# A bias product of 128 columns in place of 256, added behind the two-matrix product of its bank

## The chip, the cores and the metric

The kernel runs on one core of a Trainium2 chip. The metric is the device time of one execution in microseconds (us). Before the change three runs gave 2354.51, 2358.6 and 2351.19 us, median 2354.51.

TensorE multiplies a stationary operand (loaded by a weight load) by a moving operand and writes the result to an accumulator bank in PSUM. VectorE, ScalarE and GpSimd work on elements, SyncE (SP) issues transfers. In the profile PE is TensorE's matmul, PEld its weight load, DVE is VectorE, ACT is ScalarE and POOL is GpSimd.

## The reference

Two graph layers run over 16 graphs of 1024 nodes with 128 channels. The first is a gated network of four steps over the adjacency. The second, which the change touches, takes out some edges and then applies three SAGE passes and a linear head:

```
def _sage(x, adj, Wr, Wx, b, mf):
    deg = clip(sum(adj, axis=-1, keepdims=True), 1.0, None)
    agg = einsum('bij,bjd->bid', adj, x) / deg
    out = agg @ Wr + x @ Wx + b
    nrm = maximum(norm(out, axis=-1, keepdims=True), NORM_EPS)
    return out / nrm * mf[..., None]

h1 = bn(relu(sage(x,  adj_d, Wr1, Wx1, b1, mf)))
h2 = bn(relu(sage(h1, adj_d, Wr2, Wx2, b2, mf)))
h3 = bn(relu(sage(h2, adj_d, Wr3, Wx3, b3, mf)))
xc = concatenate([h1, h2, h3], axis=-1) * mf[..., None]
return (xc @ Wl + bl) * mf[..., None]
```

`bn` normalizes each channel over all graphs and nodes, so no graph's second pass can begin before the last graph's first pass has ended, and likewise for the third.

## The kernel before

The kernel is one program in five stages: the gated network together with the search for the edges to take out (to about 1330 us), the first pass of SAGE (to about 1890 us), the second pass (to about 2143 us), the third pass (to about 2282 us) and the head (to the end). `Sage.run` calls `first`, `second`, `third` and `last` in this order. Inside each stage, the order of the instructions on every engine is the order of the Python code: no scheduler moves them.

The batch normalization isn't applied to the data. `weights(l)` folds its scale into the weights of the next pass: `wr2` for the aggregate, and `wxp`, which holds two matrices beside each other, `Wx` of this pass and the head's part for the previous pass's output. Its shift gives a bias row: `r6` holds six rows in bfloat16, the bias of the aggregated and the plain term, each split into three parts so that their sum is exact. The matching factors of each node are in `rho`, six rows by 1024 nodes, so that the bias is a product with six rows. In `r6` only the first 128 columns are filled; the other 128 columns are set to zero once (L1276).

The work unit of the second and third passes is half a graph, 512 nodes, as four blocks of 128 nodes. `out_next(b, f)` (L1753) issues its products on TensorE:

- L1759, four products of the aggregate with `wr2`, into the bank `q_oa`.
- L1762, four bias products, with the block of `rho` stationary (6 by 128) and `r6` moving (256 columns), into the tile `q_ob`. That tile has two banks; blocks 0 and 1 share one, blocks 2 and 3 the other. The product of an even block carries the start flag, which opens its bank.
- L1765, four products of the block of `xt` with `wxp`, 256 columns in float32, which are added in the same banks. A float32 product is two records in the profile, a bfloat16 product is one. Columns 0 to 127 of a block are the pass's own term, columns 128 to 255 the head's share of the previous pass.

`chain(b, f)` (L1768) then scales the aggregate by the inverse degree (VectorE L1376 in the second pass, four ScalarE activations L1374 in the third), adds the own term (VectorE L1377), and forms the squares and their root on ScalarE (L1384, L1385). The head's share is added to an accumulator by VectorE (L1809 in the second pass, L1873 in the third), and this is what frees `q_ob`. `rows` (L1390 to L1395, VectorE) divides by the norm and applies the rectifier.

In the second pass, `slot_second(b, t)` lays out a graph in eight slots. `out_next` is in slots 0 and 3. In between TensorE turns the previous results by transposes (L1406) and aggregates the previous graph over its adjacency (L1798, float32r). The adjacency comes as bytes, unpacked by GpSimd, ScalarE and VectorE (L1749, L1751). The step that follows a unit's `out_next` is L1406 or L1798.

In the third pass, each of the 32 units i does on TensorE: the transposes (L1406) of unit i-3, then `out_next` of unit i. ScalarE copies the transposes (L1858), then does L1374, L1384 and L1385 of unit i. VectorE does `rows` of unit i-2, the statistics of unit i-3 (L1869), then L1377 and L1873 of unit i. At unit 8 a flag is formed on VectorE and TensorE (L1971 to L1977), and at unit 16 all engines load it. `q_oa`, `q_ob` and `s_tr` have two buffers there.

`load_layer` (L1716) issues on SP the loads of `q_rho`, `q_agi` and `q_xt` of a graph, in this order; each waits until the last reader of its buffer is done (two buffers in the second pass, three in the third).

The first pass has a similar sequence in `out_first` (L1565): L1571 (aggregate), L1573 (bias, six rows, 128 columns), L1576 (own term, 128 columns). It uses the same `r6`, columns 0 to 127. The head has bias products of 48 rows (L1907), behind L1899 or behind the 512-column L1903.

Of the kernel before, what the change touches and what calls it, by code (L numbers as in the profile page):

```python
# [9 lines left out]
BF = mybir.dt.bfloat16  # L10
# [11 lines left out]
P = 128  # L22
B = 16
N = 1024
C = 128
# [26 lines left out]
class Dilate:  # L52
# [15 lines left out]
    def __init__(self, ctx, tc, cst, adj, not_r):  # L68
        self.tc, self.nc, self.cst, self.adj, self.not_r = tc, tc.nc, cst, adj, not_r
        nc = self.nc  # L70
        pool = lambda name, **k: ctx.enter_context(tc.tile_pool(name=name, **k))
        self.one = pool("d_one", bufs=1)
        self.two = pool("d_two", bufs=2)
        self.small = pool("d_small", bufs=3)
        self.dram = pool("d_dram", bufs=1, space=DRAM)
        self.ps = pool("d_ps", bufs=1, space=PSUM)

        self.removed = [self.dram.tile([N, N], BF, name=f"rt{b}") for b in range(B)]

        self.coef = self.one.tile([B, ROW], F32, name="coef")
        nc.vector.memset(self.coef, 1.0)
        nc.vector.memset(self.coef[:, TAIL + 1:TAIL + 2], -1.0)
        nc.vector.memset(self.coef[:, TAIL + 2:TAIL + 3], -0.5)
        nc.vector.memset(self.coef[:, TAIL + 5:TAIL + 6], 2.0)  # L90
        self.stage = self.one.tile([P, B, ROW], BF, name="stage")
        for i, v in ((1, -8.5), (2, 1.0), (3, MAGIC), (4, -MAGIC), (5, 0.0)):
            nc.vector.memset(self.stage[:, :, TAIL + i:TAIL + i + 1], v)
        self.counts = self.one.tile([P, B, NB], F32, name="counts")
        self.free = {}
# [1101 lines left out]
class Sage:  # L1197
# [14 lines left out]
    def __init__(self, ctx, tc, cst, adj, not_r, summed, nodemask, W, vec, Wl, bl, out, bad):  # L1212
        self.tc, self.nc, self.cst = tc, tc.nc, cst
        self.adj, self.not_r, self.summed, self.out, self.bad = adj, not_r, summed, out, bad
        self.given = nodemask, W, vec, Wl, bl
        self.ctx = ctx
        pool = lambda name, **k: ctx.enter_context(tc.tile_pool(name=name, **k))
        self.one = one = pool("s_one", bufs=1)
        self.small = pool("s_small", bufs=2)
        dram = pool("s_dram", bufs=1, space=DRAM)  # L1220
        self.x1 = dram.tile([B, P, NB, C], F32, name="s_x1")
        self.at8 = dram.tile([B, 2, P, NB, HF], U8, name="s_at8")
        self.rt = dram.tile([B, 2, C, HF], F32, name="s_rt")
        self.ag = dram.tile([B, 2, C, HF], F32, name="s_ag")
        self.rho = dram.tile([B, 6, N], BF, name="s_rho")
        self.wr = one.tile([C, 3, C], F32, name="s_wr")
        self.wx = one.tile([C, 3, C], F32, name="s_wx")
        self.wl = one.tile([C, 3, C], F32, name="s_wl")

        self.vr = one.tile([10, C], F32, name="s_vr")  # L1230
        self.vt = one.tile([C, 10], F32, name="s_vt")
        self.part6 = one.tile([6, 3], F32, name="s_part6")

        self.graph = one.tile([3 * B, B], F32, name="s_graph")
        self.mask48 = one.tile([3 * B, N], BF, name="s_mask48")
        self.rdeg = one.tile([P, B, NB], F32, name="s_rdeg")
        self.stats = [one.tile([C, 2 * B, 6], F32, name=f"s_st{l}") for l in range(3)]
        self.ab = [one.tile([C, 2], F32, name=f"s_ab{l}") for l in range(3)]
        self.wr2 = one.tile([C, C], F32, name="s_wr2")
        self.wxp = one.tile([C, 2, C], F32, name="s_wxp")  # L1240
        self.r6 = one.tile([6, 2 * C], BF, name="s_r6")

    def load_given(self):

# [14 lines left out]
    def constants(self):  # L1259

        nc, ident, K = self.nc, self.cst["ident"], 3 * B
        const = self.const
        self.one16 = const([1, 1], 1.0, "s_one16", F16)

        self.sel01 = const([10, 3, 6], 0.0, "s_sel01")
        for i in range(3):
            nc.vector.tensor_copy(self.sel01[:, i, 3:], ident[:10, 3 * i:3 * i + 1].to_broadcast([10, 3]))
        self.ones = const([6, P], 1.0, "s_ones", BF)
        nc.vector.tensor_add(self.part6, ident[:6, 0:3], ident[:6, 3:6])
        self.part48 = const([K, 3], 1.0, "s_part48")  # L1270
        for base, m in ((0, 1), (B - 1, -1)):
            nc.gpsimd.affine_select(self.part48, self.part48, pattern=[[-m * B, 3]], compare_op=ALU.is_ge,
                                    fill=0.0, base=base, channel_multiplier=m)
        nc.vector.tensor_add(self.graph, ident[:K, :B], ident[:K, B:2 * B])
        nc.vector.tensor_add(self.graph, self.graph, ident[:K, 2 * B:K])
        nc.vector.memset(self.r6[:, C:], 0.0)  # L1276

        mask, junk = self.cst["mask"], self.wxp[:, 0, :].rearrange("p (a b) -> p a b", a=NB)
        nc.vector.scalar_tensor_tensor(junk, mask, 0.0, mask, op0=ALU.is_gt, op1=ALU.not_equal,
                                       accum_out=self.bad[:, BAD - 1:BAD])  # L1280

        drop = self.wr2
        nc.vector.tensor_copy(drop, ident)
        nc.vector.memset(drop[:1, :], -1.0)
        nc.vector.memset(drop[:1, :1], 0.0)
        nc.vector.memset(self.mask48[:B, :], 1.0)
# [13 lines left out]
    def const(self, shape, v, name, dt=F32):  # L1300
        t = self.one.tile(shape, dt, name=name)
        self.nc.vector.memset(t.bitcast(F32) if dt is FR else t, v)
        return t
# [30 lines left out]
    def weights(self, l, v):  # L1334

        nc = self.nc
        if l:
            self.batch_norm(l - 1)
            self.scaled(self.wr2, self.wr[:, l, :], l - 1)
            self.scaled(self.wxp[:, 0, :], self.wx[:, l, :], l - 1)  # L1340
            self.scaled(self.wxp[:, 1, :], self.wl[:, l - 1, :], l - 1)
            beta = self.small.tile([C, 2, 6], F32, name="s_beta")
            nc.vector.memset(beta, 0.0)
            for i in range(2):
                nc.vector.tensor_copy(beta[:, i, 3 * i:3 * i + 3], self.ab[l - 1][:, 1:2].to_broadcast([C, 3]))
            nc.tensor.matmul(v, beta[:, 0, :], self.wr[:, l, :], start=True, stop=False)
            nc.tensor.matmul(v, beta[:, 1, :], self.wx[:, l, :], start=False, stop=False)
        nc.tensor.matmul(v, self.sel01[:, l, :], self.vr, start=(l == 0), stop=True)
        self.parts(v, self.part6, self.r6[:, :C])

    def head_weights(self, ps):
        nc, K = self.nc, 3 * B
# [212 lines left out]
    def out_first(self, b, f):  # L1565
        nc, g = self.nc, self.g[b]
        pa = self.ps1.tile([P, 4, C], F32, name="p_oa")
        pb = self.ps1.tile([P, 4, C], F32, name="p_ob")
        ag = g["ag", f]
        for i in range(4):  # L1570
            nc.tensor.matmul(pa[:, i, :], ag[:, i * P:(i + 1) * P], self.wr[:, 0, :], start=True, stop=True)  # L1571
        for i in range(4):
            nc.tensor.matmul(pb[:, i, :], self.ones, self.r6[:, :C],  # L1573
                             start=(i == 0), stop=False)
        for i in range(4):
            nc.tensor.matmul(pb[:, i, :], g["xt", f][:, i * P:(i + 1) * P], self.wx[:, 0, :],  # L1576
                             start=False, stop=(i == 3))
        g["oa", f], g["ob", f] = pa, pb
# [174 lines left out]
    def out_next(self, b, f, ps):  # L1753
        nc, g = self.nc, self.g[b]
        pa = ps.tile([P, 4, C], F32, name="q_oa")
        pb = self.ps2.tile([P, 4, 2, C], F32, name="q_ob")
        for i in range(4):
            blk = slice(i * P, (i + 1) * P)
            nc.tensor.matmul(pa[:, i, :], g["agi"][:, f, blk], self.wr2, start=True, stop=True)  # L1759
        for i in range(4):  # L1760
            blk = slice(f * HF + i * P, f * HF + (i + 1) * P)
            nc.tensor.matmul(pb[:, i], g["rho"][:, blk], self.r6, start=(i % 2 == 0), stop=False)  # L1762
        for i in range(4):
            blk = slice(i * P, (i + 1) * P)
            nc.tensor.matmul(pb[:, i], g["xt"][:, f, blk], self.wxp, start=False, stop=(i % 2 == 1))  # L1765
        g["oa", f], g["ob", f] = pa, pb

    def chain(self, b, f, scalar=False):  # L1768
# [282 lines left out]
```

## Time and profile before

| what | value |
|---|---|
| median of three runs | 2354.51 us (2351.19 to 2358.6) |
| profiled execution: span | 2361.0 us |
| instructions in it | 35725 |
| TensorE matmul, busy | 2271.3 us, 96% |
| TensorE weight load, busy | 1567.2 us, 66% |
| VectorE, busy | 1905.5 us, 81% |
| ScalarE, busy | 1371.4 us, 58% |
| GpSimd, busy | 1027.0 us, 44% |
| L1765, 512 records | 133.0 us, mean 405 ns |
| L1759, 512 records | 71.4 us, mean 285 ns |
| L1762, 256 records | 40.1 us, mean 277 ns |
| L1573 (first pass), 128 records | 12.6 us, mean 217 ns |

The profile is of one execution, apart from the three timed runs, and only its span from first to last instruction is known. A record's length includes the time in which a matmul drains, while the next one already runs; what a matmul takes from TensorE is the distance from its start to the start of the next. In rows of the timeline the columns are: start and length in us, engine, line, operation, output and inputs, shape, number of records, and in brackets the idle time before it with the instruction that ended it. Names in the profile leave out the buffers' numbers, so `s_r` in the rows of L1762 and L1573 is `r6`. In a table by stretch, each engine's busy time stands with its number of instructions, then the granted TensorE clock as a share of full speed, the mean share of the transfer engines and the rate.

### The profile page before, as it was taken

The numbers are of one execution on the slowest core, as the hardware profiler recorded it, in microseconds if no ns is written. First come the engines' busy times: TensorE is split into PE (matmuls) and PEld (weight loads), VectorE is DVE, ScalarE is ACT, GpSimd is POOL, SyncE is SP. The second block draws the span as 40 slices with busy tenths as digits, with TensorE's granted clock in tenths as the row PEclk, the third lists the DMA queues.
The fourth block names the chain that finished last, engine by engine and source line by source line (L and its number), as shares of the span: only waits on it lengthen the run. The fifth ranks groups of instructions, "written<-read, shape, count | busy, mean of one in ns | idle before, by whom it ended". The sixth has DMA issues, their size and how long they took to land. (4 is left out here: it accounts for less than half of the span.)

```text
span 2361.0 us, 35725 instructions
## 1 busy us (share of the span) xinstructions
PE 2271.3 (96%) x11945; PEld 1567.2 (66%) x11945; DVE 1905.5 (81%) x4132; ACT 1371.4 (58%) x3206; POOL 1027.0 (44%) x964
## 2 busy tenths in 40 slices
PE   6999999999999999999999899999999989999987
PEld 4665655656665666656566577777777778887865
DVE  4998998988989989989889877777777566666777
ACT  3556565656465655556664556666566545555756
POOL 3236254253362452533532556666666435551002
PEclk9999999999999999999999899999999999999989
DMA  7327254363353372533640787778777277765414
GB/s 264 113 97 264 72 173 168 115 225 129 111 207 104 123 243 67 204 137 115 235 134 26 263 297 279 272 271 301 277 267 278 105 259 245 240 233 167 127 37 145
DMA packets 214406, 436.18 MB, mean 185 GB/s; under 512 B 59586, under 2 KB 80740, under 8 KB 214212
## 3 DMA queue, kind: packets, MB, share of 16 engines
q1 hardware_dynamic: 186244, 345.70, 42.2%
q0 software_dynamic: 23040, 83.90, 10.2%
q10 hardware_dynamic: 4928, 4.21, 0.6%
q8 instruction: 96, 1.57, 0.3%
q14 instruction: 98, 0.80, 0.1%
HBM read 324.49 MB, written 109.25 MB: 184 GB/s over the span
## 5 line engine op out<-in xcount | busy, mean ns | idle before, releaser
L1092 PE MATMUL h_g<-h_h,h_wh 128*128 128x512 f32 x768 | 397.9, 600 | 3.1 <-DVE h_r L1105 3.0
L1092 PE MATMUL h_g<-h_ms,h_wi 128*128 128x512 f32 x768 | 392.2, 593 | 0.0
L1492 POOL CAST p_b<-p_at 128x512 uint8<-128x512 f32 x256 | 257.1, 1024 | 124.2 <-ACT p_at L1485 124.2
L735 DVE TENSOR_TENSOR_SCAN f_rank<-f_a,f_first,f_pd 128x1024 f16<-128x1024 f32 x128 | 299.2, 2344 | 3.3
L1080 PE MATMUL h_g<-h_a,h_hi 128*128 128x512 f32 x1024 | 284.5, 418 | 5.7 <-DMA h_a<-in_adj_dram 5.5
L1092 PEld LDWEIGHTS h_g<-h_ms,h_wi 128*128 128x128 f32 x768 | 145.9, 190 | 183.6 <-issue 161.1
L1121 POOL TENSOR_TENSOR h_h<-h_zh,h_r 128x512 f32<-128x512 f32 x126 | 181.9, 1444 | 195.0 <-DVE h_r L1120 172.8
L1080 PE MATMUL h_g<-h_a,h_lo 128*128 128x512 f32 x1024 | 264.3, 395 | 0.0
L1485 ACT ACTIVATE p_at<-p_u,s_less 128x512 fp32r<-128x512 f32 x256 | 175.7, 688 | 146.2 <-PE p_u L1484 141.3
L1080 PEld LDWEIGHTS h_g<-h_a,h_hi 128*128 128x128 f32 x1024 | 188.6, 189 | 69.5 <-issue 20.1
L863 DVE SCALAR_TENSOR_TENSOR f_nr<-f_u,f_q,f_a 128x1024 bf16<-128x1024 f16 x128 | 183.5, 1450 | 57.4 <-ACT f_u L912 50.8
L1115 POOL TENSOR_TENSOR h_zh<-h_z,h_h 128x512 f32<-128x512 f32 x63 | 80.3, 1275 | 324.1 <-ACT h_z L1111 324.1
L1080 PEld LDWEIGHTS h_g<-h_a,h_lo 128*128 128x128 f32 x1024 | 190.2, 188 | 39.3
L1501 DVE SCALAR_TENSOR_TENSOR p_a<-p_a 128x1024 bf16<-128x1024 f32 x128 | 211.7, 1694 | 0.0
L1384 ACT ACTIVATE s_junk<-s_o 128x128 bf16<-128x128 f32 x384 | 113.8, 298 | 137.3 <-DVE s_o L1377 137.3
L1092 PEld LDWEIGHTS h_g<-h_h,h_wh 128*128 128x128 f32 x768 | 129.4, 191 | 86.1 <-issue 66.5
L1083 ACT COPY h_ms<-h_g 128x512 f32<-128x512 f32 x128 | 73.7, 576 | 174.3 <-PE h_g L1080 130.3
L1108 ACT ACTIVATE h_r<-h_r,h_bi 128x512 f32<-128x512 f32 x128 | 92.4, 722 | 138.8 <-DVE h_r L1107 138.8
L909 ACT ACTIVATE f_u<-f_rank,f_q 128x128 f16<-128x128 f16 (+7 forms) x128 | 110.6, 867 | 75.5 <-DVE f_rank L849 75.5
L1483 PE MATMUL p_u<-ident_b,p_a 128*128 128x128 bf16 x1024 | 145.4, 222 | 2.2 <-DMA p_a<-in_adj_dram 2.2
L1484 PE MATMUL p_u<-ident_b,p_nr 128*128 128x128 bf16 x1024 | 145.3, 222 | 0.0
L1765 PE MATMUL q_ob<-s_wxp,q_xt 128*128 128x256 f32 x512 | 133.0, 405 | 0.0
(258 smaller groups left out, 4950.0 us busy)
## 6 DMA issues: line engine op xcount, KB each, us to landing
h_a<-in_adj_dram POOLq DMA_DIRECT2D x128, 512.0 KB, 7.5
p_a<-in_adj_dram SPq DMA_DIRECT2D x128, 512.0 KB
f_a<-in_adj_dram SPq DMA_DIRECT2D x124, 512.0 KB
e_nr<-f_nr SPq DMA_DIRECT2D x128, 256.0 KB
p_nr<-e_nr SPq DMA_DIRECT2D x32, 1024.0 KB
s_at<-p_b SPq DMA_DIRECT2D x32, 512.0 KB
s_ag<-s_ag SPq DMA_DIRECT2D x64, 256.0 KB
q_agi<-s_ag SPq DMA_DIRECT2D x32, 512.0 KB
```

Source lines behind the costliest of these rows:

```text
L735: nc.vector.tensor_tensor_scan(out, a, other[:, 0, 0:1].to_broadcast([P, N]), start, op0=ALU.add, op1=ALU.bypass)
L863: nc.vector.scalar_tensor_tensor(nr, self.us[g], self.q[:, 2, g:g + 1], self.a[g], op0=ALU.not_equal, op1=ALU.is_ge)
L1080: nc.tensor.matmul(pm[f], part[:, j, :], st.adj[j][:, half[f]], start=(j == 0 and n == 0), stop=(j == NB - 1 and n == 1))
L1092: nc.tensor.matmul(pg, lhs, rhs, start=(i == 0), stop=(i == len(mm) - 1))
L1121: aid.tensor_tensor(h, zh, r, ALU.subtract)
L1384: self.nc.scalar.activation(junk, o[:, i, :], AF.Square, accum_out=ss[:, i:i + 1])
L1483: nc.tensor.matmul(pu[:, i * P:(i + 1) * P], a[:, blk, 1], ib, start=False, stop=False)
L1484: nc.tensor.matmul(pu[:, i * P:(i + 1) * P], nr[:, k, blk], ib, start=False, stop=(i == 3))
L1485: nc.scalar.activation(g["at"][:, j, cols], pu, AF.Relu, bias=self.less2)
L1492: self.nc.gpsimd.tensor_copy(g["b", f][:, j, :], g["at"][:, j, f * HF:(f + 1) * HF].bitcast(F32))
L1501: self.nc.vector.scalar_tensor_tensor(low, a, 0.0, a, op0=ALU.is_gt, op1=ALU.not_equal, accum_out=self.bad[:, c:c + 1])
L1765: nc.tensor.matmul(pb[:, i], g["xt"][:, f, blk], self.wxp, start=False, stop=(i % 2 == 1))
```

## The change

`r6` becomes 128 columns wide, and the memset of its second half goes. In `out_next` the two-matrix product L1765 comes in front of the bias product and carries the start flags; the bias product is 128 columns wide, goes to columns 0 to 127 of its block, and stands last, with the stop flags. The number of products is the same. Lines behind L1276 move up by one: in the changed kernel the products of `out_next` are L1758 (aggregate), L1761 (two matrices) and L1764 (bias).

```diff
@@ __init__ @@
-        self.r6 = one.tile([6, 2 * C], BF, name="s_r6")
+        self.r6 = one.tile([6, C], BF, name="s_r6")
@@ constants @@
-        nc.vector.memset(self.r6[:, C:], 0.0)
@@ weights @@
-        self.parts(v, self.part6, self.r6[:, :C])
+        self.parts(v, self.part6, self.r6)
@@ out_first @@
-            nc.tensor.matmul(pb[:, i, :], self.ones, self.r6[:, :C],
+            nc.tensor.matmul(pb[:, i, :], self.ones, self.r6,
                              start=(i == 0), stop=False)
@@ out_next @@
         for i in range(4):
+            blk = slice(i * P, (i + 1) * P)
+            nc.tensor.matmul(pb[:, i], g["xt"][:, f, blk], self.wxp, start=(i % 2 == 0), stop=False)
+        for i in range(4):
             blk = slice(f * HF + i * P, f * HF + (i + 1) * P)
-            nc.tensor.matmul(pb[:, i], g["rho"][:, blk], self.r6, start=(i % 2 == 0), stop=False)
-        for i in range(4):
-            blk = slice(i * P, (i + 1) * P)
-            nc.tensor.matmul(pb[:, i], g["xt"][:, f, blk], self.wxp, start=False, stop=(i % 2 == 1))
+            nc.tensor.matmul(pb[:, i, 0, :], g["rho"][:, blk], self.r6, start=False, stop=(i % 2 == 1))
         g["oa", f], g["ob", f] = pa, pb
```

## The prediction

> **What bounds the kernel now.** I read the page's list of groups first, then busy time by stretch, then the timeline of one unit on each engine, because one sum over 2361 us mixes stages with different limits. The two passes that change run from about 1895 to 2143 us and from 2145 to 2282 us.
>
> Busy time by stretch: the middle of the second pass, then a late stretch of the third.
>
> ```profile
> core 0: us, PE busy (x) PEld busy (x) DVE busy (x) ACT busy (x) POOL busy (x), PEclk, DMA share, GB/s
> 1905.00:2130.00 225.00, 223.31 (x1195) 184.02 (x1194) 149.93 (x274) 120.31 (x393) 110.91 (x90) 1.00 0.69 236
> 2218.00:2275.00 57.00, 56.40 (x356) 46.89 (x354) 46.60 (x106) 44.99 (x210) 0.00 (x0) 1.00 0.32 94
> ```
>
> TensorE looks full in both. Busy time can't say whether it is the bound in both, so next the timeline: one unit of the third pass on TensorE (start, length).
>
> ```profile
> 2202.19 1.06 PE L1759 MATMUL q_oa<-s_wr,q_agi 128*128 128x128 f32 x8
> 2203.18 0.61 PE L1762 MATMUL q_ob<-s_r,q_rho 6*128 6x256 bf16 x4
> 2203.71 2.00 PE L1765 MATMUL q_ob<-s_wxp,q_xt 128*128 128x256 f32 x8
> 2205.54 0.60 PE L1406 MATMUL s_tr<-ident,s_r 128*128 128x128 f32 x4
> 2205.98 1.06 PE L1759 MATMUL q_oa<-s_wr,q_agi 128*128 128x128 f32 x8
> ```
>
> A unit is 2205.98 - 2202.19 = 3.79 us with no idle time. The four bias products hold 2203.71 - 2203.18 = 0.53 us of it. Now ScalarE and VectorE in the same unit:
>
> ```profile
> 2198.96 0.31 ACT L1384 ACTIVATE s_junk<-s_o 128x128 bf16<-128x128 f32 x1 [0.76 <-DVE s_o L1377]
> ...
> 2200.27 0.21 ACT L1385 ACTIVATE s_ss<-s_ss 128x4 f32<-128x4 f32 x1
> 2200.38 0.57 ACT L1858 COPY s_r<-s_tr 128x512 f32<-128x512 f32 x1
> 2200.84 1.15 ACT L1374 ACTIVATE s_o<-q_oa,s_rdeg 128x128 f32<-128x128 f32 x4
> 2202.75 0.31 ACT L1384 ACTIVATE s_junk<-s_o 128x128 bf16<-128x128 f32 x1 [0.76 <-DVE s_o L1377]
> ```
> ```profile
> 2202.02 0.69 DVE L1377 TENSOR_TENSOR s_o<-q_ob,s_o 128x512 f32<-128x512 f32 x1 [0.35 <-ACT s_o L1374]
> ```
>
> This is a closed loop: four squares 1.31 us, root 0.11, copy 0.46, four scalings until L1377 starts 1.18, L1377 until the next square 0.73. That is 3.79 too, and ScalarE's only idle time is the wait for L1377, which itself waited for ScalarE. In this unit both are nearly tied: the bias bank is complete at 2199.92 + 2.00 = 2201.92 (L1765 of this unit started at 2199.92), L1374 ends at 2201.99. After ScalarE loses 0.76 us at the flag's load (near 2217 us) TensorE is ahead, and ScalarE's loop runs on its own:
>
> ```profile
> 2217.95 0.69 DVE L1377 TENSOR_TENSOR s_o<-q_ob,s_o 128x512 f32<-128x512 f32 x1 [0.35 <-ACT s_o L1374]
> ...
> 2270.99 0.69 DVE L1377 TENSOR_TENSOR s_o<-q_ob,s_o 128x512 f32<-128x512 f32 x1 [0.35 <-ACT s_o L1374]
> ```
>
> These are 14 units apart: 53.04 / 14 = 3.789 us. TensorE's pitch, from L1765 at 2203.71 and 18 units later at 2271.97, is 3.792 us. So the third pass is held by two loops of equal length, and the ScalarE loop contains no bias product. In the second pass the unit is 7.47 us (L1762 at 2014.09, 2021.54, 2029.04), TensorE is without gaps, ScalarE idles 2.4 to 3.5 us a unit and VectorE waits 0.58 and 0.77 us for TensorE's L1765: there TensorE alone is the bound.
>
> **What the Trainium skill says.** *TensorE: Matmul & The Clock Gate*, section Back-to-back issue gap, gives N / 2.4 + 2.5 ns between full-speed matmuls, about 109 ns for 256 columns and 56 for 128. The trace agrees: L1762's starts are 109 to 110 ns apart, L1573's (128 wide, also 6 rows) 55 to 56. The same page, step 1 of Step-by-step, says that a weight load is pulled ahead where row groups don't conflict. The trace fits: a 6-row load behind 128-row work starts only 202 ns after the last such matmul (pitch 112), while loads of equal height overlap. *PSUM — Partial Sum Buffer*, The four PSUM rules: a group's first matmul clears the has-written bits of its whole 2 KiB bank, so whichever product comes first must carry the start flag; the change moves it, two per tile as before. No trace shows these bits. The TensorE page's Part 1 has the clock halved after an idle window of some 3.4 us, free-running; here the granted clock was 0.50 from 2179.8 to 2186.6 us, after TensorE stood idle for 2.0 us.
>
> **The change part by part.** *Width.* There are 64 groups of four bias products, 32 in each pass. The first pass already has this shape:
>
> ```profile
> 1536.94 1.11 PE L1571 MATMUL p_oa<-s_wr,s_ag 128*128 128x128 f32 x8
> 1537.99 0.39 PE L1573 MATMUL p_ob<-s_r,s_ones 6*128 6x128 bf16 x4
> 1538.31 1.16 PE L1576 MATMUL p_ob<-s_wx,p_xt 128*128 128x128 f32 x8
> ```
>
> L1573 holds 1538.31 - 1537.99 = 0.32 us, L1762 holds 0.53: the difference is 4 x (109.5 - 56) = 0.214 us a group.
>
> *Place.* Entering the 6-row products costs 95 ns (207 instead of 112 after L1759; before L1907, behind a 512-wide product, 524 instead of 431: 93). Leaving costs 88 ns until the next load starts and 104 until it is done (L1765's first step is 320 instead of 216). Now L1765 follows L1759, equal rows, no switch; the switch in comes behind L1765, the switch out falls on L1406 or L1798. Two switches remain, about 0.29 us, as before. The switch out onto L1798 (fp32r) is shown nowhere: between 0 (hidden) and twice the 0.19; I take 0.19, as its load is as long. The ends are +-0.19 x 15 groups = +-2.9 us. But the bank completes sooner than TensorE moves on. From L1759's last start to completion it takes 2.74 us now (2.36 to the last L1765's start, and 0.38); then 0.11 + 7 x 0.216 + 0.31 + 0.18 + 0.22 = 2.33: 0.41 us earlier, of which 0.19 is the switch that now falls behind it.
>
> *Waits.* What waits for a free bank is now L1765, half a microsecond earlier in the unit; the bank was released 3.7 us before (L1873 of two units back), so nothing. The loads: L1762 no longer frees q_rho's buffer before L1765 frees q_xt's, so on SP's queue the load of q_rho, and q_agi behind it, issue 1.5 us later in the third pass (2203.81 and 2204.18 now, with q_xt at 2205.74). They are used four units, 15 us, later, and a load took 3.7 to 6.1 us from issue to landing in the busier second pass: nothing. Without that cover it would cost up to 1.5 us a graph. The removed memset (L1276, once, 112 ns on VectorE at 1323.9 us) is worth between 0 and 0.1 us, and I count 0; so is the smaller tile.
>
> *Second pass.* VectorE and ScalarE in turn need 14.94 - 0.77 - 0.58 = 13.59 us a graph, TensorE afterwards 14.94 - 0.43 = 14.51: still TensorE's. GpSimd's unpacked bytes are ready some 1.5 us before use. 32 x 0.214 = 6.8 us, and 0.2 because the tail hangs on the bank's completion: 7.0 us.
>
> *Third pass.* In steady state the next late thing is ScalarE's loop, which is already there: 0.004 us a unit for 14 units, 0.05 us, and TensorE idles 0.2 us a unit. It gains only where VectorE really waits for L1765 at half clock: at the start (L1377 at 2151.15) and behind the flag, where the wait of L1975 for VectorE has stopped TensorE.
>
> ```profile
> 2186.85 0.69 DVE L1377 TENSOR_TENSOR s_o<-q_ob,s_o 128x512 f32<-128x512 f32 x1 [5.12 <-PE q_ob L1765]
> ```
>
> At half clock 4 x (214 - 107) = 0.43, and 0.23 for the earlier completion: 0.66 at each, with the next unit's share some 0.7. Twice 0.7 = 1.4 us.
>
> Sum 7.0 + 1.4 = 8.4 us. The profiled execution's span, 2361.0, becomes 2352.6; it stands 6.5 us over the median of the runs, 2354.51, and I take the same 8.4 us from that: **2346.1 us**.
>
> **Rivals.** *Full gain.* The ScalarE loop is not rigid and the third pass gives its 6.8 us as well: 7.0 + 6.8 + 0.7 = 14.5, 2340.0 us. For it: TensorE's 56.40 of 57 us. Against: the fourteen units at 3.789. *Half eaten.* One or two more half-clock pieces, since TensorE now has idle time in the third pass and waits longer at the flag. A unit at half clock was 7.07 us (L1406 at 2179.49 and 2186.56) instead of 3.79, 3.3 more; one piece of 6.8 us costs 3.4: gain 5.0, 2349.5 us. The same end is reached if leaving onto L1798 costs double (gain 5.5). *Slower.* The clock stays halved in the third pass, because TensorE waits in each unit: 3.3 us a unit. Break-even is 8.4 / 3.3 = 2.5 units; with 5 units 2354.5 + 8.1 = 2362.6 us. Against: from 2293 to 2350 us TensorE has 1.5 us idle in 57 and the clock is 1.00. *No effect of the width*, if the 93 ns weight load set the pitch: 2353, spoken against by L1573's 56 ns.
>
> **How the numbers follow.** My case 0.62, own range 2343 to 2349 (three runs of the kernel before span 7.4 us); full gain 0.12; half eaten or no width effect 0.22; slower 0.04. About 0.3%, 7 us, is what a measurement here can tell. My case lies just beyond it and reaches beyond it three times in four: 0.47, with 0.12 and 0.01 makes faster 0.60; same 0.36; slower 0.04. Range 2340 to 2351 takes in the full gain and most of the half eaten.
>
> **What would show it.** Bias products 56 ns apart and their group 0.32 us long; second pass's unit 7.26 us; the third pass's unit still 3.79, with TensorE idle some 0.2 us a unit ahead of L1406, waiting for L1395. A third-pass unit of 3.58 would refute the loop; clock pieces at 0.5 between 2190 and 2275 would point to the eaten gain; a longer first step of L1798 to the switch.

## The result

The changed kernel takes 2347.98 us (median of six runs, 2345.36 to 2349.54) against 2356.56 us of the kernel before (six runs, 2351.19 to 2364.55). The ratio is 0.9955, 95% interval 0.9939 to 0.9972: 0.45% faster, 8.6 us by the medians. The profiled execution's span fell from 2361.0 to 2346.2 us. On a second chip, with 31 runs of the kernel before, the ratio was 0.9948 (0.9934 to 0.9963).

Below is the profile after, view by view. Busy time by stretch, the middle of the second pass and a late stretch of the third (columns as before):

```profile
core 0: us, PE busy (x) PEld busy (x) DVE busy (x) ACT busy (x) POOL busy (x), PEclk, DMA share, GB/s
1912.00:2122.00 210.00, 210.00 (x1161) 172.54 (x1160) 141.88 (x261) 116.35 (x380) 105.70 (x86) 1.00 0.72 246
2204.00:2260.00 56.00, 51.93 (x349) 42.33 (x347) 45.88 (x105) 44.61 (x209) 0.00 (x0) 1.00 0.31 96
```

The two passes have come apart. TensorE is still full in the second, but idles 56.00 - 51.93 = 4.07 us in 56 of the third, at full clock. Both stretches leave out the start of the second pass, where the granted clock was 0.50 for a while. First the kernel before:

```profile
1893.00:1903.30 10.30, 8.51 (x29) 6.80 (x30) 3.52 (x10) 0.92 (x7) 0.00 (x0) 0.50 1.01 380
```

Then the changed kernel:

```profile
1891.50:1898.30 6.80, 4.59 (x16) 3.98 (x16) 2.56 (x9) 0.00 (x0) 0.00 (x0) 0.50 1.01 355
1898.30:1908.60 10.30, 7.98 (x52) 6.07 (x51) 6.99 (x14) 5.15 (x22) 2.10 (x2) 1.00 0.77 302
1908.60:1912.00 3.40, 3.40 (x11) 2.65 (x11) 3.05 (x5) 1.18 (x7) 3.40 (x4) 0.50 0.99 252
```

The half clock comes in two pieces instead of one, and the first ends sooner after the pass's first product. Next the timeline of the second pass on TensorE:

```profile
2003.84 0.39 PE L1764 MATMUL q_ob<-s_r,q_rho 6*128 6x128 bf16 x4
2004.16 2.12 PE L1797 MATMUL q_ag<-q_at,q_rh 128*128 128x512 f32 x8
...
2009.30 1.89 PE L1761 MATMUL q_ob<-s_wxp,q_xt 128*128 128x256 f32 x8
2011.12 0.39 PE L1764 MATMUL q_ob<-s_r,q_rho 6*128 6x128 bf16 x4
2011.45 0.65 PE L1405 MATMUL s_tr<-ident,s_r 128*128 128x128 f32 x4
```

The bias products hold TensorE for 0.32 to 0.33 us, not 0.53. Over 22 units in the middle of the pass the unit is 7.234 us on average, where it was 7.473. The third pass's unit on TensorE:

```profile
2190.31 0.63 PE L1405 MATMUL s_tr<-ident,s_r 128*128 128x128 f32 x4 [0.22 <-DVE s_r L1394]
2190.77 1.06 PE L1758 MATMUL q_oa<-s_wr,q_agi 128*128 128x128 f32 x8
2191.67 1.89 PE L1761 MATMUL q_ob<-s_wxp,q_xt 128*128 128x256 f32 x8
2193.49 0.39 PE L1764 MATMUL q_ob<-s_r,q_rho 6*128 6x128 bf16 x4
2194.10 0.63 PE L1405 MATMUL s_tr<-ident,s_r 128*128 128x128 f32 x4 [0.22 <-DVE s_r L1394]
```

It is 2194.10 - 2190.31 = 3.79 us, as before. The time that the narrower product saves is now a wait: the transposes wait 0.22 us in each unit for VectorE's L1394 (L1395 before). ScalarE's loop is unchanged:

```profile
2184.59 0.31 ACT L1383 ACTIVATE s_junk<-s_o 128x128 bf16<-128x128 f32 x1 [0.76 <-DVE s_o L1376]
...
2188.39 0.31 ACT L1383 ACTIVATE s_junk<-s_o 128x128 bf16<-128x128 f32 x1 [0.76 <-DVE s_o L1376]
```

2188.39 - 2184.59 is 3.80 us. VectorE's additions, 14 units apart as before:

```profile
2203.59 0.69 DVE L1376 TENSOR_TENSOR s_o<-q_ob,s_o 128x512 f32<-128x512 f32 x1 [0.35 <-ACT s_o L1373]
...
2256.70 0.69 DVE L1376 TENSOR_TENSOR s_o<-q_ob,s_o 128x512 f32<-128x512 f32 x1 [0.35 <-ACT s_o L1373]
```

53.11 / 14 = 3.794 us. The addition behind the flag (L1376 at 2172.49 us), which had waited 5.12 us for TensorE, now waits 3.31.

Where the 14.8 us between the two spans lie: 1.0 before the second pass's first aggregate product (work that the change doesn't touch), 7.7 from there to the third pass's first (250.11 us before, 242.38 after), 5.6 from there to the head's first product (136.4 and 130.9), 0.5 at the end. The runs' medians show less, 8.6 to 10.3 us; one part of the third pass's 5.6 us belongs to the profiled execution of the kernel before alone. There the pass's start fell almost wholly into half clock, and its first addition came 6.25 us after its first product; in the two other traces with the bias product in front (e4_before_loop, e9_before_flag below) the start ran at full clock and took 4.04 us. So 2.2 us differ from execution to execution. The stop at the flag was followed by 6.8 us of half clock before and by 3.4 us after; the two additions around it lie 9.34 us apart before and 7.36 us after. This difference of 2.0 us recurs: 9.27 us in e4_before_loop, 7.37 us when the changed kernel was profiled again (e0_after).

### The profile page after: what moved, and what is told of

It is laid out like the page before. It is cut to its first block, busy times and chain, and to the rows that moved or that the text cites. A ratio compares the mean times of both kernels' runs of the same rounds, so it can differ in the third digit from the quotient of the medians.

```text
span 2346.2 us, 35711 instructions
## 1 busy us (share of the span) xinstructions
PE 2249.2 (96%) x11945; PEld 1546.2 (66%) x11945; DVE 1905.8 (81%) x4131; ACT 1372.5 (58%) x3206; POOL 1030.4 (44%) x964
## 3 DMA queue, kind: packets, MB, share of 16 engines
q0 software_dynamic: 23040, 83.90, 10.2%
## 5 line engine op out<-in xcount | busy, mean ns | idle before, releaser
L886 ACT ACTIVATE f_pd<-f_rank,f_q 128x128 f32<-128x128 f16 x128 | 59.1, 462 | 112.6 <-DVE f_q L697 109.4
```

## The experiments

All times are medians. The first four ran on one chip beside 31 runs of the kernel before (2358.36 us), the next four on another beside 19 (2358.18), the last two on a third beside 33 (2359.19).

### The changed kernel again (e0_after)

No edit.

> The changed kernel itself once more, on the chip of the next three. Theory: 8 to 11 us under the kernel before (about 2347), units of 7.24 us in the second pass and 3.79 us in the third. Rival (the gain of the profile was a matter of which stretches ran at half clock): under 4 us.

Measured: 2348.08 us, 10.3 under the kernel before; units 7.233 and 3.789 us. The gain is confirmed and the rival falls.

### The place alone (e2_order)

```diff
 (changed kernel)
-        self.r6 = one.tile([6, C], BF, name="s_r6")
+        self.r6 = one.tile([6, 2 * C], BF, name="s_r6")
+        nc.vector.memset(self.r6[:, C:], 0.0)
...
-            nc.tensor.matmul(pb[:, i, 0, :], g["rho"][:, blk], self.r6, ...)
+            nc.tensor.matmul(pb[:, i], g["rho"][:, blk], self.r6, ...)
```

> The place alone: the two-matrix product opens the bank, the bias product stays 256 columns wide, with its zero half, and comes last. Theory (the width is the gain): the unit of the second pass stays at 7.44 to 7.48 us, the bank completes some 0.2 us earlier, in all 0.5 to 2 us under the kernel before. Rival (the place is the gain, because two switches of row height fall elsewhere): unit 7.24 us, 8 us or more under the kernel before.

Measured: 2355.47 us, 2.9 under the kernel before (ratio 0.998, 0.9971 to 0.999); second pass's unit 7.447 us, third's 3.79. On TensorE:

```profile
2009.78 1.89 PE L1762 MATMUL q_ob<-s_wxp,q_xt 128*128 128x256 f32 x8
2011.60 0.61 PE L1765 MATMUL q_ob<-s_r,q_rho 6*128 6x256 bf16 x4
2012.14 0.66 PE L1406 MATMUL s_tr<-ident,s_r 128*128 128x128 f32 x4
```

The group is 2012.14 - 2011.60 = 0.54 us long again. From here to the changed kernel only the width changes: 7.447 - 7.233 = 0.214 us a unit, to the nanosecond what was worked out, and 7.4 us in the runs. The place saves 0.027 us a unit, because leaving the six-row products onto L1406 costs less than onto L1765: the first step of L1406 is 164 ns against the usual 109, an excess of 55, where L1765's was 320 against 216, 104. Only every other unit gains: those ahead of L1406 fall from 7.451 to 7.399 us, those ahead of L1798 stay (7.496 and 7.495). But 0.027 x 32 is 0.9 us, and the runs show more than the expected 0.5 to 2. The last two experiments follow that up. The width alone, with the bias product still in front, wasn't tried.

### A shorter loop on ScalarE (e3_after_loop, e4_before_loop)

```diff
 (third; the same edit to the changed kernel and to the kernel before)
-                    nc.scalar.copy(self.r3[:, b2, f2, :], pt)
+                    keep = lambda ...: nc.scalar.copy(self.r3[:, b2, f2, :], pt)
...
-                if i >= 3:
-                    nc.vector.bn_stats(self.stats[2][...], self.r3[:, b2, f2, :])
                 if i < len(units):
-                    pp = self.chain(b, f, True)
+                    pp = self.chain(b, f, True, keep)   # scalings, keep(), squares
                     nc.vector.tensor_add(acc, pp, acc)
+                if i >= 3:
+                    nc.vector.bn_stats(self.stats[2][...], self.r3[:, b2, f2, :])
```

> The changed kernel with the third pass's ScalarE loop shortened by 0.46 us and no work left out: ScalarE's copy of the transposes (and VectorE's statistics behind it) move from ahead of the scalings into the wait for VectorE's addition, ahead of the squares. Theory (ScalarE's loop of 3.79 us holds the third pass, TensorE would need 3.53): unit 3.53 to 3.58 us, 6 to 8 us under the changed kernel. Rival (TensorE, or plain occupancy of ScalarE and VectorE, holds it): unit stays 3.79, within 1 us of the changed kernel.

> The kernel before with the same shortened ScalarE loop. Theory: TensorE's own unit of 3.79 us is now the only bound of the third pass, so 3.79 stays and the time is within 1.5 us of the kernel before. Rival (the reordering saves time by itself, whatever TensorE does): unit below 3.7, 4 us or more under the kernel before.

Measured: from the changed kernel 2340.50 us, 7.6 under it on the same chip, unit 3.53 to 3.56 us late in the pass. From the kernel before 2359.54 us, no change (ratio 1.0005, 0.9996 to 1.0014), unit 3.79. ScalarE in the first of them:

```profile
2218.82 0.21 ACT L1384 ACTIVATE s_ss<-s_ss 128x4 f32<-128x4 f32 x1
2218.93 1.12 ACT L1373 ACTIVATE s_o<-q_oa,s_rdeg 128x128 f32<-128x128 f32 x4
2219.93 0.61 ACT L1859 COPY s_r<-s_tr 128x512 f32<-128x512 f32 x1
2220.82 0.31 ACT L1383 ACTIVATE s_junk<-s_o 128x128 bf16<-128x128 f32 x1 [0.27 <-DVE s_o L1376]
```

The copy L1859 now fills the wait for the addition, of which 0.27 us is left. And VectorE's addition waits for TensorE's bias product again (in all, times, longest):

```profile
DVE s_o L1376 <- PE q_ob L1764: 10.3, 19, 2.3
```

In the kernel before, with the loop shortened, TensorE is back to back at its old length, 2218.83 - 2215.04 = 3.79 us:

```profile
2215.04 0.60 PE L1406 MATMUL s_tr<-ident,s_r 128*128 128x128 f32 x4
...
2218.83 0.62 PE L1406 MATMUL s_tr<-ident,s_r 128*128 128x128 f32 x4
```

So two loops of the same length held the third pass. Shortening either one alone leaves its unit at 3.79 us; shortening both gives the 7 us that the width is worth in that pass. Both rivals fall. The edit moves VectorE's statistics along with ScalarE's copy, and the two weren't tried apart; but VectorE waited 0.35 us for ScalarE in each unit of the changed kernel, so VectorE itself had time to spare.

### The switches doubled, and taken out (e1b_switch, e5_rows)

```diff
 (out_next of the changed kernel, e1b_switch)
+        for h in range(2):
+            (two-matrix products of blocks 2h and 2h + 1)
+            (bias products of blocks 2h and 2h + 1)
```
```diff
 (changed kernel, e5_rows)
+        self.r6w = one.tile([P, C], BF, name="s_r6")     # zeroed once
+        self.r6 = self.r6w[:6, :]
+        self.rho3 = [accp.tile([P, N], BF, name=f"q_rho{i}") for i in range(3)]   # zeroed once
...
-        g["rho"] = pool.tile([6, N], BF, name="q_rho")
-        nc.sync.dma_start(g["rho"], self.rho[b])
+        g["rho"] = self.rho3[(b + self.turn) % 3]
+        nc.sync.dma_start(g["rho"][:6, :], self.rho[b])
...
-            nc.tensor.matmul(pb[:, i, 0, :], g["rho"][:, blk], self.r6, ...)
+            nc.tensor.matmul(pb[:, i, 0, :], g["rho"][:, blk], self.r6w, ...)
```

> The changed kernel with the switches of row height doubled: the two bias products of a bank come directly behind its two two-matrix products, so that a group enters and leaves the six-row products twice. Theory (a pair of switches costs 0.25 to 0.29 us, and placing them can only move, not remove it): unit of the second pass 7.48 to 7.53 us, TensorE's unit in the third 3.79 to 3.82, 8 to 10 us over the changed kernel, the whole gain gone. Rival (switches are hidden behind the 256-column products): unit 7.24, within 1 us of the changed kernel.

> The changed kernel with no switch: the bias factors and the bias rows stand in tiles of 128 rows whose rows 6 to 127 are zero (three tiles zeroed once by GpSimd, kept over both passes); the sum is the same. Theory (unequal row height, not bfloat16 or the small size, makes the switch): unit of the second pass 6.95 to 7.00 us, third pass still 3.79, 7 to 9 us under the changed kernel. Rival (the change from float32 to bfloat16 is what costs): unit 7.24, within 1 us of the changed kernel.

Measured: doubled, 2357.45 us, the unit 7.530 us, 9.4 over the changed kernel (of the other chip) and level with the kernel before (0.9995, 0.9986 to 1.0004). Taken out, 2340.16 us, TensorE's unit 6.990 us, 7.9 under the changed kernel (of the other chip; 32 units give 7.8); the third pass's unit stays 3.79. A group with doubled switches on TensorE:

```profile
2006.52 1.03 PE L1762 MATMUL q_ob<-s_wxp,q_xt 128*128 128x256 f32 x4
2007.48 0.28 PE L1765 MATMUL q_ob<-s_r,q_rho 6*128 6x128 bf16 x2
2007.69 1.13 PE L1762 MATMUL q_ob<-s_wxp,q_xt 128*128 128x256 f32 x4
2008.76 0.28 PE L1765 MATMUL q_ob<-s_r,q_rho 6*128 6x128 bf16 x2
2008.97 2.11 PE L1798 MATMUL q_ag<-q_at,q_rh 128*128 128x512 f32 x8
```

And with 128 rows:

```profile
2009.41 1.89 PE L1763 MATMUL q_ob<-s_wxp,q_xt 128*128 128x256 f32 x8
2011.14 0.39 PE L1766 MATMUL q_ob<-s_r,q_rho 128*128 128x128 bf16 x4
2011.36 0.61 PE L1407 MATMUL s_tr<-ident,s_r 128*128 128x128 f32 x4
```

Here four products hold TensorE for 0.22 us, and the step into them is 216 ns, not 311. A pair of switches is worth 0.24 us where the way out falls on L1405 or L1797 (7.233 - 6.990), and 0.30 us where it falls on the two-matrix product (7.530 - 7.233). It is the unequal row height: the products stayed in bfloat16 and the switch vanished. How unequal height makes the cost no run shows.

### The later flag (e7_flag)

```diff
 (third, changed kernel)
                 if i == 8:
-                    pt = self.ps2.tile([P, 4, P], F32, name="s_tr")
-                    flag = flagged(nc, self.one, pt[:1, 0, :1], self.bad)
+                    later = flagged(nc, self.one, self.bad)        # VectorE's part
+                if i == 10:
+                    pt = self.ps2.tile([P, 4, P], F32, name="s_tr")
+                    flag = later(pt[:1, 0, :1])                    # TensorE's product
```

> The changed kernel with the flag's product on TensorE two units later than the VectorE operations that it needs, so that TensorE doesn't stop at unit 8 of the third pass. Theory (the gap of 7.37 us between two additions there is a wait of TensorE and the half clock behind it): the gap falls to 3.8 us, no piece of half clock there, 3 to 4 us under the changed kernel. Rival (the clock piece only moves elsewhere): within 1 us of the changed kernel.

Measured: 2346.07 us, 2.0 under the changed kernel's 2348.08 (of another chip). The runs of the two overlap (2344.08 to 2348.94 and 2344.74 to 2349.29), so they tell this gain neither from none nor from the 3 us expected. In the trace the gap is gone:

```profile
2164.13 0.69 DVE L1376 TENSOR_TENSOR s_o<-q_ob,s_o 128x512 f32<-128x512 f32 x1 [0.35 <-ACT s_o L1373]
2167.92 0.69 DVE L1376 TENSOR_TENSOR s_o<-q_ob,s_o 128x512 f32<-128x512 f32 x1 [0.35 <-ACT s_o L1373]
```

These are units 7 and 8, 3.79 us apart (7.37 in the changed kernel), and no half clock follows. From the second pass's first product to the head's first the trace is 3.5 us shorter than that of the changed kernel (369.75 and 373.23), so the half clock hasn't moved elsewhere. The mechanism is shown by the trace; the gain in the runs' times isn't.

### All three (e8_all)

Edit: e3_after_loop, e5_rows and e7_flag together.

> The changed kernel with all three: no switch, the shortened ScalarE loop, the later flag. Theory: second pass 6.97 us a unit; third pass held by the shortened ScalarE loop of 3.33 us, TensorE needing 3.26 to 3.28; flag 3.5 us: 24 to 27 us under the changed kernel, about 2322. Rival (VectorE or ScalarE becomes the bound of the second pass, or VectorE's own order that of the third): unit of the third 3.5 or more, or of the second over 7.05, and less than 19 us.

Measured: 2328.15 us, ratio to the kernel before 0.987 (0.9853 to 0.9887), 30.0 us under it and 19.9 under the changed kernel. Second pass's unit 6.990 us, near the 6.97 expected; the third's 3.41 us late in the pass, not 3.33. TensorE's unit without gaps is 3.31 us, not 3.26 to 3.28. ScalarE's loop and TensorE take turns in holding the pass: VectorE's addition waits for the one, then for the other.

```profile
2190.61 0.69 DVE L1378 TENSOR_TENSOR s_o<-q_ob,s_o 128x512 f32<-128x512 f32 x1 [0.21 <-ACT s_o L1375]
...
2194.12 0.69 DVE L1378 TENSOR_TENSOR s_o<-q_ob,s_o 128x512 f32<-128x512 f32 x1 [0.42 <-PE q_ob L1766]
```

The sum of the parts was estimated too high, but this is the fastest of the kernels run.

### Where the place saves (e9_before_flag, e10_order_flag)

Edit: the later flag, in the kernel before and in e2_order.

> The kernel before with the later flag product. Theory: the gap at unit 8 falls from 9.34 to 3.79 us, 3 to 5.5 us under the kernel before. Rival (the lost time at half clock turns up elsewhere): under 1.5 us.

> The bias product behind, still 256 columns wide, with the later flag product. Theory (what the place alone gave beyond 1 us came from the stop at the flag): 0.5 to 2 us under the kernel before with the later flag. Rival (the place saves in the passes themselves or at their start): still 3 us or more under it.

Measured: 2354.92 us, 4.3 under the kernel before, as expected, with the gap at 3.79 us; and 2350.91 us. The place gives 4.0 us without the flag's stop too: the expectation falls, the rival stands. In the traces the largest piece is at the start of the second pass, which runs at half clock. TensorE with the bias product in front (e9_before_flag), then behind (e10_order_flag):

```profile
1891.87 2.05 PE L1759 MATMUL q_oa<-s_wr,q_agi 128*128 128x128 f32 x8 [1.59 <-DVE s_r L1332]
1893.85 1.03 PE L1762 MATMUL q_ob<-s_r,q_rho 6*128 6x256 bf16 x4
1894.81 3.78 PE L1765 MATMUL q_ob<-s_wxp,q_xt 128*128 128x256 f32 x8
1898.38 1.25 PE L1759 MATMUL q_oa<-s_wr,q_agi 128*128 128x128 f32 x8
```
```profile
1893.52 2.05 PE L1759 MATMUL q_oa<-s_wr,q_agi 128*128 128x128 f32 x8 [2.12 <-DVE s_r L1332]
1895.37 3.26 PE L1762 MATMUL q_ob<-s_wxp,q_xt 128*128 128x256 f32 x8
1898.56 0.61 PE L1765 MATMUL q_ob<-s_r,q_rho 6*128 6x256 bf16 x4
1899.09 1.16 PE L1759 MATMUL q_oa<-s_wr,q_agi 128*128 128x128 f32 x8
```

The first group, from L1759 to the next L1759, takes 6.51 us in front and 5.57 behind, with the same products. The first addition comes 6.82 us after the first aggregate product in e9_before_flag and 5.73 in e10_order_flag; it was 6.81 to 6.82 in all three traces with the bias product in front and 5.0 to 5.9 in all nine with it behind. In e9_before_flag the half clock there lasts 10.2 us and covers the whole first group, in e10_order_flag it lasts 6.8 us and ends inside it.

At the third pass's start the same distance is 4.04 and 3.59 us, at full clock. Nearly half of this is a wait that the old order had. The bias rows `r6` are the last thing that VectorE writes before the pass, and the bias product in front stood waiting for them, in e9_before_flag:

```profile
2143.29 0.59 PE L1762 MATMUL q_ob<-s_r,q_rho 6*128 6x256 bf16 x4 [0.21 <-DVE s_r L1332]
```

Behind, in e10_order_flag, the two-matrix product runs in that time and the bias product doesn't wait:

```profile
2144.40 0.60 PE L1765 MATMUL q_ob<-s_r,q_rho 6*128 6x256 bf16 x4
```

From the second pass's first product to the head's first the two traces differ by 2.7 us (378.31 and 375.63). The runs' 4.0 us needn't be more than that: the intervals of the two ratios to the kernel before, 0.9974 to 0.9992 and 0.9955 to 0.9979, overlap.

## Why the prediction was right

The time was forecast as 2346.1 us and measured as 2347.98, a gain of 8.4 us against 8.6 (10.3 on the second chip). The mechanism held; that forecast and medians agree to 0.2 us is luck. The ratio's interval allows a gain of 6.6 to 14.4 us, so it is the units in the traces that tell the cases apart, not the time. And in the traces the parts add up to more than was counted: 7.3 to 7.7 us in the second pass, 0.7 at the third pass's start and 2.0 at the flag, where 7.0, 0.7 and 0.7 were forecast. Step by step:

**Width.** The 0.214 us a group, taken from the first pass's L1573, held exactly (e2_order against e0_after).

**Place.** "Two switches remain, as before" held in the main: doubling and removing them moved the unit by 0.30 and 0.24 us, against the 0.29 counted. Onto L1798 (L1797) the switch cost what was taken: those units kept their length in e2_order. Onto L1406 (L1405) it cost 0.05 us less, which makes the mean unit 0.027 us shorter than forecast, 7.233 and not 7.26. The other mis-sized term is the earlier completion of the bank: 0.2 us were counted for it, at the tail, and none for the pass's start at half clock, where the place alone made the first addition 1.1 us earlier. The second pass's gain was put at 7.0 us and was 7.7 from first product to first product (7.3 in e0_after). Why a switch costs time stays open: the prediction explains it by row groups that conflict, but loads of equal height use the same rows and overlap all the same. That unequal height makes the cost is shown by e5_rows.

**Waits and loads.** The bank's release and the later loads cost nothing, as said: TensorE has no gap in the middle of the second pass, and in the steady third waits only for L1394.

**Third pass.** The claim that two loops of equal length hold it, and that the width therefore gives nothing there, is what decided between 8.4 and 14.5 us. It is shown three ways: the unit stayed 3.79 with 0.22 us of waiting, the shorter loop brought the 7.6 us forth, and the same loop brought nothing without the width. Of the two restarts, counted at 0.7 us each, the first came out in size, but not by its working. That had half clock, 0.43 us for the width and 0.23 for the place. At full clock the first addition came 4.04 us after the first product in e4_before_loop and e9_before_flag, 3.59 with the place alone and 3.38 in the changed kernel: 0.45 for the place, 0.21 of it the wait for `r6` that the prediction didn't see, and 0.21 for the width. The second is mis-sized: the gap at the flag fell by 2.0 us (9.34 and 9.27 to 7.36 and 7.37), together with the half clock behind it, from 6.8 to 3.4 us. Why that piece became shorter is open.

**The rivals.** The full gain didn't come, for the reason given. Slower, and half eaten in its main form, rested on TensorE's new waits halving the clock; it stayed at 1.00 with 4.07 us idle in 56. TensorE did wait longer at the flag, 3.22 us where it was 1.97, yet less half clock followed. Both waits are shorter than the 3.4 us of idle time that the prediction cites for a halved clock, and after 2.18 us in e2_order none followed: here the measurements decide, and the length of the wait alone doesn't. One new piece of 3.4 us did come, at the start of the second pass (1908.6 to 1912.0 us), but the piece ahead of it was 3.4 us shorter. Leaving onto L1798 didn't cost double. That the width has no effect falls with e2_order. The forecast stood just beyond the 0.3% that can be told, and the measured 0.45% lies just beyond it too.

## What to carry to other kernels

Before the saving of a full engine is multiplied by its units, close the other engines' loops in each stage: add up the steps from one instruction to itself a unit later, waits included. Where that sum equalled the full engine's pitch here, shortening either alone left the unit as it was, and the pair of edits gave all of it. The cheapest edit of such a loop is to put independent work of the same engine into its wait, as with the copy here.

The product with 6 rows between products of 128 rows paid for two switches in each of the three places where it was tried. Padding its operands with zero rows showed no cost of its own here and gave more in the second pass than halving its width (0.24 us a unit against 0.21).

## What the runs showed of the hardware

- A pair of switches between weight loads of 6 and of 128 rows costs TensorE 0.24 to 0.30 us at full clock, by what comes behind it (e5_rows, after, e1b_switch). With equal rows the step into the bfloat16 products is 216 ns in place of 311, no longer than any other step of the product ahead of them.
- At the second pass's start, TensorE's half clock lasted 10.2 us in all three traces with the bias product in front and 6.8 us in all nine with it behind. Five of these nine (after, e0_after, e3_after_loop, e7_flag and e1b_switch) had another 3.4 us of it some 10.3 us later; the other four had none. Idle time at the switches inside the first group doesn't account for it alone: e1b_switch has a pair inside the group as well, and its half clock lasted 6.8 us. The cause is open.
- Waits of 0.2 us in each unit of 3.79 us didn't lower the granted clock over 56 us.
